# Three edits to a two-layer graph network: groups of x, one more early product, the order of the last group

## The chip, the core and the metric

The kernel runs on one core of a Trainium2 chip. Its engines run side by side, each with a queue of its own, and wait for each other by semaphores: PE multiplies matrices and writes to PSUM, DVE and ACT work element by element, POOL issues the gathers (indirect DMAs that fetch rows by index), SP issues the other DMAs. The metric is the time of one execution on the device in microseconds, as the median of several runs.

## The reference

x has N = 6250 rows (nodes) of D = 512, float32; src and dst are the E = 100,000 edges, sorted by dst. What is computed:

```python
h = jnp.maximum(_layernorm(x, axis=-1), 0.0)
# norm = -dinv[src] * dinv[dst], dinv = 1/sqrt(degree by src), 0 without edges
def prop(h):
    return jax.ops.segment_sum(h[src] * norm[:, None], dst, num_segments=N)
h = h @ W1_0 + prop(h) @ W1_1 + b1
h = _layer_norm(h, gamma, beta)
h = jnp.where(h >= 0, h, 0.01 * h)
return x + h @ W2_0 + prop(h) @ W2_1 + b2
```

So each of two layers multiplies the nodes' own rows by one matrix (W0 below) and the sums over their edges by another (W1), both 512 x 512.

## The kernel before, in words

**Tiles.** Nodes lie in NB = 49 blocks of 128 rows (the last has 106). Edges lie in NC = 782 chunks of 128. A chunk is fetched by one gather of 128 rows of 2 KB (L393 of `gather_to`) into one of R = 57 places in SBUF, in turn: chunk t goes into place `order[t % 57]`. Sixteen places are extra ones, the other 41 hold blocks 0 to 40 of x at first; the blocks behind them hold x too, and later, from the middle of layer 1, the second layer's weights.

**Sums.** Four lists of chunks make a group: list q of group g has three chunks of its own and the next list's first, so a full group is 16 products of a 128 x 32 selection matrix `sel` (made by DVE in `choose`, L504 and L515) with a gathered chunk, in `sums` (L527). The profile shows each float32 product as two records. The four lists write to four column groups of PE and lie side by side there. There are NS = 66 groups: group 0 has one list, the groups 1 to 64 have four, and group 65 has four lists of 4, 4, 4 and 2 chunks (771 to 774, 774 to 777, 777 to 780, 780 and 781), so 14 products and 28 records. ACT copies a group's sums to `agg` (L530).

**Blocks.** The rows of a group are nodes in order, but not aligned with blocks. `place` (L533 on) turns them into a block's transposed sums: for every group that may hold rows of the block (`inside[i]`, two or three groups) DVE writes a 0/1 matrix `there` (L540) and PE multiplies it with the group's `agg` in four parts (L543, eight records). DVE then scales the result into aT (L594). `own` transposes the block's own rows (L466) and ACT copies them (hT, L468). `dense` makes hT times W0 and aT times W1 in one PSUM tile (L478), and `finish` adds the bias, normalises, and stores: in layer 1 to a table tab[1] in DRAM, which layer 2 gathers from, and to h_tab; in layer 2 to the output.

**Order.** PE, POOL and SP issue in the order of the program; DVE's and ACT's order comes from the scheduler. For every group g the program issues the gathers up to chunk 3 * unit[g] + 57, the places of the blocks that are due, the sums of g, and the dense products of those blocks. A gather waits until the sums have used the chunk that lay in its place. The first gather of layer 2 needs all of tab[1]. Blocks 38 to 48 are due at groups 54, 55, 56, 58, 59, 60, 62, 63, 64, and, for 47 and 48, after the loops of groups 64 and 65; at groups 53 and 57 no block is due.

**Early blocks.** For three blocks, `EARLY`, W0 is not multiplied in `dense` but in `early`, at group 55 for block 46, 57 for 47 and 59 for 48, behind the sums and dense products of that group. Their rows are loaded two groups before (`load_early`) into tiles `pre`, one for each early block, which then hold the product with its bias until `finish` adds it.

**The start.** x is loaded into its places in groups of blocks (L165 on); ACT makes the sums and squares of the first 41 blocks, DVE counts degrees until some 85 us. When the scale of every row is known (93.9 us), `make_table` writes the normalised x of each group in place, on ACT (L407) or DVE (L404 and L405), and SP writes it to tab[0] in DRAM (L408). The first 60 chunks (RAW) are gathered from raw x, not from that table, and are normalised in SBUF: `find` and `look_up` (L418 to L444: PE, DVE, then ACT) fetch each row's scale. A gather into a place that holds a block of x waits until that block's group has been written to tab[0], so chunk 16 + i waits for the group of block i. Chunks from 60 on wait for the whole table.

Before the first group, `usual_path` makes table group 0 and group 1 on ACT, between them the loads for the first two blocks, and four look-ups. Then, at group 0:

```python
more_tables(1, [DVE])
gather_to(layer, RE + groups[3][0])
```

Then come the sums of group 0, the next table group (DVE and ACT by turns, block by block), a look-up, and all other table groups.

Of the kernel before, what the change touches and what calls it, by code (L numbers as in the profile page):

```python
# [8 lines left out]
F32 = mybir.dt.float32  # L9
# [10 lines left out]
P = 128  # L20
# [9 lines left out]
RE = 16  # L30
# [9 lines left out]
def gnn_kernel(  # L40
# [36 lines left out]
    NB = -(-N // P)  # L77
# [4 lines left out]
    NC = -(-E // P)  # L82
# [3 lines left out]
    NS = -(-NU // NQ)  # L86
# [65 lines left out]
    for ids, fill, name in ((src, 0, "src_c"), (dst, NO_NODE, "dst_c")):  # L152
        t = ep.tile([P, NG, P], I32, name=name)
# [11 lines left out]

    groups, i = [], 0
    while i < NB:
        n = min(NB - i, (2, 6, 8)[len(groups)] if len(groups) < 3 else 7)
        groups.append((i, n))
        i += n  # L170
    xs = []
    for i0, n in groups:
        t = places[:, i0 : i0 + n, :]
# [32 lines left out]
    with tc.tile_pool(name="turn", bufs=1) as wp, tc.tile_pool(  # L206
        name="turn_ps", bufs=2, space=bass.MemoryType.PSUM
# [17 lines left out]
    for (i0, n), t in zip(groups, xs):  # L225
        n = min(n, NB - LAST - i0)
# [13 lines left out]
    with tc.tile_pool(name="deg", bufs=1) as dp, tc.tile_pool(name="onehot", bufs=2) as ohp, tc.tile_pool(  # L240
        name="deg_ps", bufs=1, space=bass.MemoryType.PSUM
# [10 lines left out]
        for g in range(EJ // (2 * GJ)):  # L252
            hot = []
            for s, n, name in ((s_lo, LO, "lo"), (s_hi, HI, "hi")):
                t = ohp.tile([EP, GJ, n, 2], BF, name=name)
# [23 lines left out]
    with tc.tile_pool(name="fold", bufs=1) as dp, tc.tile_pool(  # L279
        name="fold_ps", bufs=1, space=bass.MemoryType.PSUM  # L280
# [27 lines left out]
    with tc.tile_pool(name="turn", bufs=1) as wp, tc.tile_pool(  # L308
        name="turn_ps", bufs=1, space=bass.MemoryType.PSUM
# [50 lines left out]
def usual_path(tc, have):  # L360
# [5 lines left out]
                          "minus unsorted ln dinv sdinv bias1 bias2 gam bet unseen unit N E D NB NC NU NS KD rows places "  # L366
                          "order groups xs sc pick src_lo src_hi p_id dup").split())
    AHEAD = 2
    EARLY = {NB - 3: NS - 11, NB - 2: NS - 9, NB - 1: NS - 7}
    ACT = mybir.EngineType.Activation  # L370
    R = len(order)
    UN = STEP * P * N / E
# [7 lines left out]
    with ExitStack() as es:  # L380
        pool = es.enter_context(tc.tile_pool(name="main", bufs=2))
# [5 lines left out]
        def zr(t):  # L387
            return places[:, order[t % R], :]

        def gather_to(layer, end):  # L390
            nonlocal gathered
            for t in range(gathered, min(end, NC)):
                nc.gpsimd.indirect_dma_start(  # L393
                    out=zr(t), out_offset=None, in_=x if layer == 0 and t < RAW else tab[layer],
                    in_offset=bass.IndirectOffsetOnAxis(ap=sidx[:, t : t + 1], axis=0))
            gathered = max(gathered, min(end, NC))

        def make_table(g, engines):

            i0, n = groups[g]  # L400
            for j in range(n):
                i, v = i0 + j, xs[g][:, j, :]
                if engines[i % len(engines)] == DVE:
                    nc.vector.tensor_scalar(v, v, sc[:, 0, i : i + 1], sc[:, 1, i : i + 1], op0=OP.mult, op1=OP.add)  # L404
                    nc.vector.tensor_scalar_max(v, v, 0.0)  # L405
                else:
                    nc.scalar.activation(v, v, AF.Relu, bias=sc[:, 1, i : i + 1], scale=sc[:, 0, i : i + 1])  # L407
            nc.sync.dma_start(tab[0][i0 * P : (i0 + n) * P, :].rearrange("(i p) d -> p i d", p=P), xs[g])  # L408
# [43 lines left out]
        def load(layer, i):  # L452

            if i not in EARLY:
                load_h(layer, i, "h", AHEAD)
# [25 lines left out]
        def load_early(layer, i):  # L481
            load_h(layer, i, "pre", len(EARLY))
            pre[i] = own_h[i]
            if layer == 1:
                load_x(i)
# [33 lines left out]
        def sums(g, sel, chunk):  # L519

            n = len(chunk)
            ps = psum.tile([P, D], F32, name="ps")
            todo = [(s, q) for s in range(SPAN) for q in range(n) if s < len(chunk[q])]
            if g == NS - 1:
                todo.sort(key=lambda t: chunk[t[1]][t[0]])
            for s, q in todo:
                nc.tensor.matmul(ps[q * Q : (q + 1) * Q, :], sel[:, q, s, :], zr(chunk[q][s]), start=(s == 0),  # L527
                                 stop=(s == len(chunk[q]) - 1))
            agg[g] = pool.tile([P, D], F32, name="agg", bufs=3)
            nc.scalar.activation(agg[g][: n * Q], ps[: n * Q], AF.Copy)  # L530

        def place(i, some):

            r = rows[i]
            if i not in placed:
                placed[i] = psum.tile([P, KD, P], F32, name="aT_ps", bufs=1)
            for g in some:
                m = Q * (unit[g + 1] - unit[g])
                there = pool.tile([P, P], F32, name="there", bufs=3)
                nc.vector.tensor_scalar(there[:m, :r], iota_r[:m, :r], node_of[:m, g : g + 1], -(1.0 + i * P),  # L540
                                        op0=OP.subtract, op1=OP.is_equal)
                for kc in range(KD):
                    nc.tensor.matmul(placed[i][:, kc, :r], agg[g][:m, kc * P : (kc + 1) * P], there[:m, :r],  # L543
                                     start=(g == inside[i][0] and kc == 0),
                                     stop=(g == inside[i][-1] and kc == KD - 1))

        def finish(layer, i, v):
            r = rows[i]
            v = v[:r]
            if layer == 1:  # L550
                o = pool.tile([P, D], F32, name="t")
                if i in EARLY:
                    nc.vector.tensor_add(o[:r], v, pre.pop(i)[:r])
# [6 lines left out]
            if i < NB - 1:  # L560
                nc.vector.tensor_add(v, v, pre.pop(i)[:r] if i in EARLY else bias1[:r])  # L561
            st = pool.tile([P, 6], F32, name="st")
# [21 lines left out]
        def turn(layer, i):  # L584

            r = rows[i]
            if layer == 1 and i not in EARLY:
                load_x(i)
            if i + AHEAD < NB:
                load(layer, i + AHEAD)  # L590
            hT = None if i in EARLY else own(layer, i)
            place(i, [g for g in inside[i] if i < NB - 1 or g == NS - 1])
# [61 lines left out]
        for i in range(AHEAD):  # L654
            load(0, i)
        make_table(1, [ACT])
        for k in range(RE // 4):
            look_up("u_ps")
            find("ps")
        tables = 2  # L660

        def more_tables(n, engines):
            nonlocal tables
# [4 lines left out]
        for layer in range(2):  # L668
            if layer == 1:
                gathered = 0  # L670
                for i in range(AHEAD):
                    load(layer, i)
            i = 0
            for g in range(NS):
                if layer == 0 and g == 0:
                    more_tables(1, [DVE])
                    gather_to(layer, RE + groups[3][0])
                else:
                    gather_to(layer, STEP * unit[g] + R)
                if layer == 0 and g == NS // 2:  # L680
                    for k, w in enumerate((W2_1, W2_0)):
                        nc.sync.dma_start(w_late[:, k], w.rearrange("(k p) d -> p k d", p=P))
                if layer == 0:
                    look_up("hT_ps")
                    find("hT_ps")
                    assert looked >= min(RAW, STEP * unit[g + 1] + 1)
                due = []
                while inside[i].stop <= g:
                    due.append((i, turn(layer, i)))
                    i += 1  # L690
                if g == NS - 2:
                    for k, (hT, aT) in due:
                        dense(layer, k, hT, aT)
                    due = []
                sums(g, *(chosen if g == NS - 1 else choose(g)))
                if layer == 0:
                    if g == 0:
                        more_tables(1, [DVE, ACT])
                    look_up("hT_ps")
                    find("hT_ps")  # L700
                    if g == 0:
                        more_tables(len(groups), [DVE, ACT])
                for k, (hT, aT) in due:
                    dense(layer, k, hT, aT)
                if layer == 0:
                    look_up("hT_ps")
                    find("hT_ps")
                    if g == NS // 2:
                        check()
                for k, at in EARLY.items():  # L710
                    if g == at - 2:
                        load_early(layer, k)
                    if g == at:
                        early(layer, k)
                if g == NS - 2:
                    chosen = choose(NS - 1)
                    if layer == 0:
                        r = rows[NB - 1]
                        started[NB - 1] = psum.tile([P, D], F32, name="u_ps")
                        nc.tensor.matmul(started[NB - 1][:r], ident[:r, :r], pre[NB - 1][:r], start=True, stop=False)  # L720
                    while inside[i].stop < NS:
                        dense(layer, i, *turn(layer, i))
                        i += 1
                    assert i == NB - 1
                    place(i, inside[i][:-1])
            dense(layer, i, *turn(layer, i))
# [322 lines left out]
```

## Time and profile before

| | |
|---|---|
| median of the runs | 2531.47 us (2527.57, 2531.47, 2532.97) |
| the profiled execution | 2509.83 us, its span 2508.0 us |
| mean granted clock of PE | 0.885 |
| layer 1: first gather into a place that held x | 99.18 us |
| layer 1: last gather | 1239.7 us |
| layer 2: first gather | 1310.31 us |
| layer 2: last gather | 2440 us |
| a gather on POOL (L393) | 0.95 us busy |
| sums of a full group, 32 records, while POOL pauses | 3.57 us |
| a block's place, 24 records, while POOL pauses | 2.7 us |
| W0 or W1 of one block, 8 records, while POOL pauses | 3.5 to 3.7 us |

The profile is one execution. Its rows name an instruction by line, engine, operation and tiles; "idle before" says how long the engine had nothing to run just before, and which event ended that. The chain is followed back from the last instruction: each step goes to what released it. "Issue" is idle time for which the profile shows no cause. PE's rows show when a product is started; their ends are modelled, and when another engine sees the result can be later.

### The profile page before, as it was taken

How to read it: one execution, taken by the hardware profiler on the slowest of the kernel's cores; microseconds unless marked ns; L12 is line 12 of the kernel's file. 1: busy time of each engine (PE TensorE's matmuls, PEld its weight loads, DVE VectorE, ACT ScalarE, POOL GpSimd, SP SyncE). 2: the span in 40 equal slices, each digit the busy share in tenths (PEclk: the TensorE clock that was granted, in tenths of full speed). 3: DMA queues.
4: the chain of work that ended last, by engine and by line, in shares of the span. 5: the costliest groups of instructions: out<-in, count | busy, mean ns of one | idle time of the engine just before them, and what ended most of it. 6: DMA issues, size and time to landing. Idle time of an engine off the chain costs nothing.

```text
span 2508.0 us, 24149 instructions
## 1 busy us (share of the span) xinstructions
PE 1948.0 (78%) x9101; PEld 913.8 (36%) x9101; DVE 691.2 (28%) x1381; ACT 377.3 (15%) x694; POOL 1496.6 (60%) x1577
## 2 busy tenths in 40 slices
PE   5617788688888888887874568887888888688888
PEld 4414343243334334333430233333333333343344
DVE  8923223232324223323340011111111111111221
ACT  8724111111111111112110000000000000000000
POOL 4175666666666666665507566666666666666660
PEclk8757899899999999999996679998998989889999
DMA  9395677767677677776627567677676777677770
GB/s 341 102 336 152 213 228 217 213 209 223 211 220 256 208 223 222 215 224 214 188 70 214 178 201 225 208 229 221 218 226 212 221 212 221 211 214 236 220 225 28
DMA packets 198947, 527.08 MB, mean 210 GB/s; under 512 B 31864, under 2 KB 46019, under 8 KB 198822
## 3 DMA queue, kind: packets, MB, share of 16 engines
q0 software_dynamic: 125120, 410.09, 53.7%
q1 hardware_dynamic: 73702, 115.36, 13.3%
q8 instruction: 73, 1.20, 0.2%
q14 instruction: 52, 0.43, 0.1%
HBM read 474.06 MB, written 51.27 MB: 209 GB/s over the span
## 4 chain that ended last, share of the span: by engine, by line
PE 67%; issue 17%; another core or an unknown queue 5%; DVE 5%; POOL 3%; DMA 2%; ACT 1%; SPq 0%; POOLq 0%; DVEq 0%; ACTq 0%
PE u_ps L478 26%; PE ps L527 25%; PE aT_ps L543 13%; POOL places L393 3%; PE hT_ps L466 2%; DMA places<-tab,sidx 1%; DVE hi L256 1%; DVE lo L256 1%; DVE places L404 0%; DVE places L405 0%; ACT agg L530 0%; PE both_ps L262 0%; PE u_ps L433 0%; PE hT_ps L433 0%
## 5 line engine op out<-in xcount | busy, mean ns | idle before, releaser
L393 POOL DMA_INDIRECT places<-tab,sidx x1504 | 1421.8, 945 | 844.3 <-issue 395.5
L527 PE MATMUL ps<-places,sel 128*32 128x512 f32 x4168 | 734.2, 649 | 158.8 <-issue 108.9
L543 PE MATMUL aT_ps<-there,agg 128*128 128x128 f32 (+2 forms) x2320 | 381.7, 313 | 207.4 <-issue 191.8
L543 PEld LDWEIGHTS aT_ps<-there,agg 128*128 128x128 f32 (+1 forms) x2320 | 340.2, 222 | 245.7 <-issue 224.0
L527 PEld LDWEIGHTS ps<-places,sel 128*32 128x32 f32 x4168 | 165.9, 117 | 647.6 <-issue 585.7
L515 DVE TENSOR_TENSOR sel<-dlx,nodes_ps 128x512 f32<-128x512 f32 (+3 forms) x134 | 89.7, 671 | 804.9 <-remote 513.6
L530 ACT ACTIVATE agg<-ps 128x512 f32<-128x512 f32 (+1 forms) x132 | 78.7, 596 | 1206.2 <-remote 632.1
L478 PE MATMUL u_ps<-w,hT 128*128 128x512 f32 (+1 forms) x392 | 189.7, 616 | 25.4 <-issue 15.9
L478 PE MATMUL u_ps<-places,hT 128*128 128x512 f32 (+1 forms) x392 | 185.7, 611 | 14.7 <-ACT hT L468 7.6
L478 PE MATMUL u_ps<-w,aT 128*128 128x512 f32 (+1 forms) x392 | 181.1, 596 | 13.8 <-issue 9.8
L478 PE MATMUL u_ps<-places,aT 128*128 128x512 f32 (+1 forms) x392 | 177.9, 593 | 6.6 <-issue 4.2
L540 DVE TENSOR_SCALAR there<-iota_r,node_of 128x128 f32<-128x128 f32 (+1 forms) x290 | 84.1, 293 | 340.0 <-remote 184.3
L478 PEld LDWEIGHTS u_ps<-w,hT 128*128 128x128 f32 (+1 forms) x392 | 71.7, 192 | 140.6 <-issue 121.0
L478 PEld LDWEIGHTS u_ps<-places,hT 128*128 128x128 f32 (+1 forms) x392 | 70.7, 190 | 127.3 <-issue 119.4
L478 PEld LDWEIGHTS u_ps<-w,aT 128*128 128x128 f32 (+1 forms) x392 | 73.1, 189 | 114.3 <-issue 108.9
L478 PEld LDWEIGHTS u_ps<-places,aT 128*128 128x128 f32 (+1 forms) x392 | 73.9, 189 | 101.7 <-issue 98.7
L594 DVE TENSOR_TENSOR aT<-aT_ps,to 128x512 f32<-128x512 f32 (+1 forms) x98 | 67.3, 687 | 150.9 <-PE ps L527 117.5
L393 POOL DMA_INDIRECT places<-in_x_dram,sidx x44 | 44.2, 1005 | 90.3 <-ACT places L407 58.8
L468 ACT ACTIVATE hT<-hT_ps 128x512 f32<-128x512 f32 (+1 forms) x98 | 58.1, 593 | 246.7 <-PE hT_ps L466 69.8
L561 DVE TENSOR_TENSOR u_ps<-u_ps,bias 128x512 f32<-128x512 f32 x46 | 32.2, 700 | 190.7 <-PE u_ps L478 86.1
L555 DVE TENSOR_TENSOR u_ps<-u_ps,bias 128x512 f32<-128x512 f32 x46 | 32.1, 699 | 183.2 <-PE u_ps L478 92.1
L463 ACT ACTIVATE h<-h,ln 128x512 f32<-128x512 f32 x46 | 37.2, 812 | 256.4 <-issue 131.0
(138 smaller groups left out, 963.7 us busy)
## 6 DMA issues: line engine op xcount, KB each, us to landing
places<-tab,sidx POOLq DMA_INDIRECT x1504
tab<-t SPq DMA_DIRECT2D x48, 256.0 KB
h_tab<-g SPq DMA_DIRECT2D x48, 256.0 KB
xt<-in_x_dram SPq DMA_DIRECT2D x48, 256.0 KB
out_dram<-t SPq DMA_DIRECT2D x48, 256.0 KB
h<-in_x_dram SPq DMA_DIRECT2D x46, 256.0 KB
h<-h_tab SPq DMA_DIRECT2D x46, 256.0 KB
places<-in_x_dram SPq DMA_DIRECT2D x4, 1792.0 KB
```

The lines of the kernel that those rows point to most:

```text
L256: nc.vector.tensor_tensor(t, s[:, g * 2 * GJ : (g + 1) * 2 * GJ].rearrange("p (j s) -> p j s", s=2)[:, :, None, :] .to_broadcast([EP, GJ, ...
L393: nc.gpsimd.indirect_dma_start(out=zr(t), out_offset=None, in_=x if layer == 0 and t < RAW else tab[layer], in_offset=bass.IndirectOffsetO ...
L463: nc.scalar.activation(h[:r], h[:r], AF.Relu, bias=ln[:r, 1, i : i + 1], scale=ln[:r, 0, i : i + 1])
L466: nc.tensor.transpose(ps[:, kc, :r], h[:r, kc * P : (kc + 1) * P], ident[:r, :r])
L468: nc.scalar.activation(hT[:, :, :r], ps[:, :, :r], AF.Copy)
L478: nc.tensor.matmul(u_ps[:r], hT[:, kc, :r], w[:, kc, :], start=(start and kc == 0), stop=(stop and kc == KD - 1))
L515: nc.vector.tensor_tensor(sel[:, q : q + k, :w, :], of, node[:, q : q + k, None, :].to_broadcast([P, k, w, Q]), op=OP.is_equal)
L527: nc.tensor.matmul(ps[q * Q : (q + 1) * Q, :], sel[:, q, s, :], zr(chunk[q][s]), start=(s == 0), stop=(s == len(chunk[q]) - 1))
L530: nc.scalar.activation(agg[g][: n * Q], ps[: n * Q], AF.Copy)
L540: nc.vector.tensor_scalar(there[:m, :r], iota_r[:m, :r], node_of[:m, g : g + 1], -(1.0 + i * P), op0=OP.subtract, op1=OP.is_equal)
L543: nc.tensor.matmul(placed[i][:, kc, :r], agg[g][:m, kc * P : (kc + 1) * P], there[:m, :r], start=(g == inside[i][0] and kc == 0), stop=(g ...
L594: nc.vector.tensor_tensor(aT[:, :, :r], placed.pop(i)[:, :, :r], to.pop(i)[:, None, :r].to_broadcast([P, KD, r]), op=OP.mult)
```

## The change

Three things are changed, and one buffer is taken away.

First, x comes in groups of 2, 4, 4, 4 and five of 7 blocks, where it came in 2, 6, 8, four of 7 and one of 5. The three first groups (10 blocks) are made into the table by ACT before group 0, where two (8 blocks) were; the group that DVE makes before the sums of group 0 has 4 blocks, where it had 8. The gathers issued there end at chunk 30 instead of 32, since `groups[tables][0]` is 14 where `groups[3][0]` was 16. SP issues nine loads of x and nine table writes instead of eight.

Second, block 45 becomes an early block: its W0 is multiplied at group 53, its rows are loaded at group 51. `pre` has four tiles instead of three, and `there` two instead of three, so the third matrix of a block can be written when PE has used the first.

Third, the products of group 65 are sorted by max(chunk, 779) instead of by chunk. The first eleven, chunks 771 to 779, then keep the order of the other groups (first chunk of every list, then the second, and so on, as far as they are below 780); chunk 780 follows for lists 3 and 2, and chunk 781.

```diff
-        n = min(NB - i, (2, 6, 8)[len(groups)] if len(groups) < 3 else 7)
+        n = min(NB - i, (2, 4, 4, 4)[len(groups)] if len(groups) < 4 else 7)
...
-    EARLY = {NB - 3: NS - 11, NB - 2: NS - 9, NB - 1: NS - 7}
+    EARLY = {NB - 4: NS - 13, NB - 3: NS - 11, NB - 2: NS - 9, NB - 1: NS - 7}
...
             if g == NS - 1:
-                todo.sort(key=lambda t: chunk[t[1]][t[0]])
+                todo.sort(key=lambda t: max(chunk[t[1]][t[0]], NC - 3))
...
-                there = pool.tile([P, P], F32, name="there", bufs=3)
+                there = pool.tile([P, P], F32, name="there", bufs=2)
...
         make_table(1, [ACT])
+        make_table(2, [ACT])
         for k in range(RE // 4):
             look_up("u_ps")
             find("ps")
-        tables = 2
+        tables = 3
...
                     more_tables(1, [DVE])
-                    gather_to(layer, RE + groups[3][0])
+                    gather_to(layer, RE + groups[tables][0])
```

## The prediction

> **What bounds the kernel now.** I read the page's rows of busy time and the chain first, then the timelines of POOL, PE and DVE, then the chain stretch by stretch.
>
> ```profile
> PE 1948.0 (78%) x9101; PEld 913.8 (36%) x9101; DVE 691.2 (28%) x1381; ACT 377.3 (15%) x694; POOL 1496.6 (60%) x1577
> ...
> PE 67%; issue 17%; another core or an unknown queue 5%; DVE 5%; POOL 3%; DMA 2%; ACT 1%; SPq 0%; POOLq 0%; DVEq 0%; ACTq 0%
> ...
> L393 POOL DMA_INDIRECT places<-tab,sidx x1504 | 1421.8, 945 | 844.3 <-issue 395.5
> L527 PE MATMUL ps<-places,sel 128*32 128x512 f32 x4168 | 734.2, 649 | 158.8 <-issue 108.9
> ```
>
> PE carries two thirds of the chain, but it and POOL hold each other. A gather takes 0.95 us and 0.30 us of issue, 1.25 us in all; POOL runs 10 to 14 of them, stops for 2.2 to 2.9 us until the sums of a group free places, and runs again. Sums that lie four groups apart start at 741.9, 810.0, 879.3, 950.0, 1018.1 and 1088.9: 68 to 71 us for 48 gathers, which alone take 60 us. PE's own work for the same four groups, at the durations it has while POOL pauses, is some 45 us; in the later part of each POOL run it gets one record started every 0.7 or 1.4 us. No view names what holds it. So three stages are judged apart: the start, where POOL waits for x's places; the steady part; and the ends of both layers, after the last gather, where PE is alone and every microsecond of it counts.
>
> The start, in POOL's timeline (chunks 18, 24 and 30):
>
> ```profile
> 100.42 0.95 POOL L393 DMA_INDIRECT places<-in_x_dram,sidx  x1 [0.30 <-issue]
> 113.77 0.95 POOL L393 DMA_INDIRECT places<-in_x_dram,sidx  x1 [12.40 <-ACT places L444]
> ...
> 128.23 1.03 POOL L393 DMA_INDIRECT places<-in_x_dram,sidx  x1 [6.63 <-DVE ac L442]
> ...
> 136.47 0.94 POOL L393 DMA_INDIRECT places<-in_x_dram,sidx  x1 [0.30 <-DVE both L439]
> ```
>
> POOL lost 12.40 and 6.63 us here. The releasers named had other work; what POOL waited for are the table's writes, as a place may be overwritten only when its block of x has been written out: group 1 (6 blocks) was issued at 103.90 and landed at 111 to 113, group 2 (8 blocks, made by DVE) was issued at 117.16 and landed at 127.45. From 128.23 POOL runs unbroken to 189.9. The chain behind it:
>
> ```profile
> 141.73 18.01 another core or an unknown queue
> 159.76 0.69 DVE sel L515
> 160.45 20.99 another core or an unknown queue
> ```
>
> That is PE, held back under POOL's long run; the sums of group 2 start only at 200.23, after it.
>
> The end of layer 1, in the chain:
>
> ```profile
> 1258.21 0.44 PE hT_ps L466 x4
> ...
> 1279.77 3.57 PE ps L527 x32
> ...
> 1291.52 5.38 PE ps L527 x28
> ```
>
> **1. Groups of x.** The loads: ACT's statistics end at 78.2, after which ACT is idle until 92; DVE's counting, to 85, sets that stage, so loads of another size are worth 0. If that cover went, one load's wait (1.43 us before group 1's statistics) is the price. One x load and one table write more cost SP 0.37 us each (the median of L408's DMAs), beside other work. The tables: chunks 18 to 29 now need groups 1 to 3, of 4 blocks each. Group 1's write, 1 MB, is issued at 103.9; 1.5 MB took 7.08 us to its main part, so it lands between 108.6 (in proportion) and 111.0 (same time). Groups 2 (ACT, ready by 104.9) and 3 (DVE, whose first four pairs of L404 and L405 end at 104.3) follow at once and land, by the same bytes per time, by 112 and 115; chunk 26 would reach group 3 only at about 119. So POOL resumes at 110 to 112 instead of 113.77 and makes twelve gathers, to 125 or 127. Chunk 30 needs group 4 (7 blocks): DVE makes it after the first selection, to about 121 (7 pairs at 0.46 + 0.34 us), and its write lands about 5 to 6 us later, 126.5. Chunk 30 starts at 126.5 to 128 instead of 136.47: 8.5 to 10 us earlier. All of this reaches the end only if PE's sums follow. The sums of group 1 (138 to 142) and the look-ups have so far run before PE was held back; if that begins earlier, part of them falls into it. Ends: −10 and +3 (ACT's later table takes one block more, and the sums of group 1 may be caught). I take −6, nearer the gain, because the gathers up to chunk 72 need nothing from PE but the sums of groups 0 and 1.
>
> The Trainium skill, "DMA: Bandwidth & Descriptors", Bandwidth, speaks against smaller writes: it wants at least 1 MiB in a DMA and gives 1 MB 6.15 us, 78% of peak. By that figure group 1 lands at 110.1, in between my two bounds; the sum goes by the bounds.
>
> **2. Block 45's W0 in group 53.** In each layer's tail four transposes (0.44 us) and eight records of W0 (1264.83 to 1268.37, 3.53 us) go: −4.0 us, all on the chain, since POOL's last gather is at 1239.7 and DVE and ACT wait for PE. They come back after the sums of group 53 (1088.9 to 1092.6), where no block is due. PE there does 4.1 us more and waits for ACT's copy of hT between; in the three blocks treated so already that wait was 3.21, about 1 and 2.19 us. The price in the lock-step: a stretch of four groups without such a block takes 69.0 to 69.3 us, with one 72.6, with two 71.3 or 69.7, alike in both layers: 3.5, 1.1 and 0.3 us for each, 1.6 on average. So −2.4 us a layer, −4.8 in all. Ends: free, −8; all of 4.1 + 3.2 us paid, +3.3 a layer, +6.6. The block's load, at group 51, has two groups (some 35 us) to land, in a buffer of its own; behind it on SP stand only loads for later blocks.
>
> **3. Last group.** Fourteen products take 5.38 us, sixteen of a full group 3.57. The old order (by chunk) sends one list's products behind each other: counting four column groups that run side by side and one queued each gives six rounds of 0.89 us, 5.4. The new order takes the first eleven by turn of the lists, then chunks 780 and 781: four rounds, 3.57. −1.8 us a layer, −3.6 in all. Every gather landed some 45 us before (1243 against 1291.5), so the order makes nothing wait. Late next is the copy by ACT (0.60), as before. Ends: −4.4 (another half round each) and 0.
>
> **4. Two buffers for `there`.** This adds a wait. With three, a block's matrices are all written before its place begins: the lead is 9 us at least. With two, the third matrix waits until PE has used the block's first. DVE's order stays, and at the spot where it now waits it waited before for that same use (there for the next block's matrix); so DVE loses nothing and what stands behind (`sel`, aT, the finish) moves only if PE does. PE could lose. I compared, for all blocks, the end of the write that stands at that spot now with the start of PE's third part. Around 1050, in PE's timeline and in DVE's:
>
> ```profile
> 1047.97 2.84 PE L543 MATMUL aT_ps<-there,agg 128*128 128x128 f32 x24
> ```
> ```profile
> 1051.22 0.48 DVE L540 TENSOR_SCALAR there<-iota_r,node_of 128x128 f32<-128x128 f32 x1 [0.75 <-PE aT_ps L543]
> ...
> 1055.46 0.29 DVE L540 TENSOR_SCALAR there<-iota_r,node_of 128x128 f32<-128x128 f32 x1 [2.88 <-remote]
> ...
> 1059.69 0.69 DVE L594 TENSOR_TENSOR aT<-aT_ps,to 128x512 f32<-128x512 f32 x1 [3.27 <-remote]
> ```
>
> PE's rows start the third part at 1049.76, the matrix would be there at 1051.70: 1.9 us late, which is also the median of 89 such places, 227 us in all. That is the upper end. But the same rows show PE's uses *complete* far behind the records: DVE sees the first done at 1051.2, the second at 1055.4, the third at 1059.7. A matrix that comes at 1051.70 is 3.8 us ahead of the second's completion. In 79 of 89 places it is ahead by 0.3 us or more (median 1.2); in ten it comes with it, and costs about one write, 0.28 us. I take +2 (0 to +227), by the rows of completion.
>
> On PE's running ahead, the Trainium skill, "TensorE: Matmul & The Clock Gate", Back-to-back issue gap, speaks of a 64-deep reorder window; 33 records (with weight loads, 66) lie here between a use and its completion, which fits, and a wait inside a block takes this lead from PE.
>
> **Sum.** −6 − 4.8 − 3.6 + 2 = −12.4. The profiled execution (2509.83 us, span 2508.0) becomes 2497; it lies 21.6 us under the median of the runs, 2531.47, so I put the same difference there: 2519.
>
> **Rivals.** *A, given back (22%):* PE's hold in the start begins as much earlier as POOL does, and group 53 pays its work in full instead of a fourth; only the last group stays, with the waits: −3.6 + 2 = −1.6, 2530. For it: a hold that has no named cause may go with the gathers' number. Against: the steady part pays 1.6 us for such work. *B, slower (20%), the third matrix:* PE's lead over its completions is what carries it through POOL's runs, and each mid-block wait is paid at the rate of PE work in group 53's like, 1.6 of 6.1 us, a fourth: 227 / 4 = 57. 2531.5 − 14.4 + 57 = 2574. It decides from a sixteenth of the 227 on (14.4 us). For it: the late arrivals recur in nearly every block. Against: the completion rows. *C, everything (8%):* start −10, W0 free: −10 − 8 − 3.6 = −21.6, 2510. The forecast itself (2513 to 2526) has 50%.
>
> **How the numbers follow.** A measurement tells 0.2% (5 us) from no change. Faster by more: forecast and C less what reaches the edge, 55%; within: A, 22%; slower: B and the worst of A, 23%. Range: below to C with 2 us of the runs' spread, 2508; above into B to a tenth of its late arrivals plus the open start (2531.5 − 8 + 23), 2547, which leaves 15% above and 4% below.
>
> **What would show it.** Chunk 30's gather near 127 and the sums of group 2 near 192 (start); the last group's 28 records in 3.6 us; no W0 between 1258 and 1270 less the shift, and groups 52 to 56 within 73 us; PE rows of L543 with idle time released by DVE L540 below 5 us in all. Wrong if four steady groups take over 70 us throughout (B), or if the sums of group 2 stay near 200 (A).

## The result and the profile after

The changed kernel takes 2596.96 us (2583.93 to 2603.68, four runs), the kernel before 2529.52 us beside it (2519.07 to 2532.97): a ratio of 1.027, 95% interval 1.0241 to 1.0298. The prediction was 2519 us, faster; the change is 67 us slower. Its profiled execution took 2594.12 us, with a span of 2592.3 us and a mean granted clock of 0.846 where it was 0.885.

The page of the changed kernel, the same rows as shown of before and the row of the places' products beside them:

```profile
PE 1903.8 (73%) x9101; PEld 919.2 (35%) x9101; DVE 692.4 (27%) x1377; ACT 380.9 (15%) x698; POOL 1504.4 (58%) x1577
...
PE 57%; issue 17%; another core or an unknown queue 13%; DVE 7%; POOL 3%; DMA 2%; ACT 1%; SPq 0%; POOLq 0%; ACTq 0%; DVEq 0%
...
L393 POOL DMA_INDIRECT places<-tab,sidx x1504 | 1425.6, 948 | 936.6 <-issue 394.1
L527 PE MATMUL ps<-places,sel 128*32 128x512 f32 x4168 | 658.7, 703 | 77.1 <-issue 40.3
L543 PE MATMUL aT_ps<-there,agg 128*128 128x128 f32 (+2 forms) x2320 | 411.5, 327 | 412.2 <-issue 286.1
```

and that last row on the page of the kernel before:

```profile
L543 PE MATMUL aT_ps<-there,agg 128*128 128x128 f32 (+2 forms) x2320 | 381.7, 313 | 207.4 <-issue 191.8
```

The last number ahead of the arrow is PE's idle time just before these instructions. Before L543 it was 207.4 us and is 412.2; before L527 it was 158.8 and is 77.1. So PE now stands still longer ahead of the places, and less in the sums behind them, which makes up for part of it. The table says where the 84 us between the two profiled executions arose, by the start of a group's sums:

| sums of group | layer 1, before | after | later by | layer 2, later by |
|---|---|---|---|---|
| 2 | 200.2 | 186.1 | −14.1 | |
| 5 | 249.6 | 245.4 | −4.2 | 51.3 |
| 21 | 531.4 | 545.9 | 14.5 | 55.2 |
| 37 | 810.0 | 842.7 | 32.7 | 72.0 |
| 53 | 1088.9 | 1133.6 | 44.7 | 77.9 |
| 61 | 1232.8 | 1286.5 | 53.7 | 88.4 |
| 65 | 1291.4 | 1343.2 | 51.8 | 86.0 |

The start is earlier, the ends of both layers shrink, and between them the kernel loses a little in most stretches of groups. From group 33 to group 53 of layer 1, four groups take 71.8 to 78.5 us where they took 68.1 to 70.8: the prediction's sign for its rival B. What is lost shows best in layer 2, in PE's timeline and in DVE's (start, duration, what, and idle before it):

```profile
1676.76 1.95 PE L543 MATMUL aT_ps<-there,agg 128*128 128x128 f32 x16
1684.21 2.04 PE L543 MATMUL aT_ps<-there,agg 128*128 128x128 f32 x8 [5.50 <-issue]
1686.18 5.77 PE L527 MATMUL ps<-places,sel 128*32 128x512 f32 x32
...
1699.29 1.95 PE L543 MATMUL aT_ps<-there,agg 128*128 128x128 f32 x16
1707.32 2.05 PE L543 MATMUL aT_ps<-there,agg 128*128 128x128 f32 x8 [6.08 <-issue]
```
```profile
1679.45 0.69 DVE L556 TENSOR_TENSOR t<-u_ps,xt 128x512 f32<-128x512 f32 x1
1683.78 0.28 DVE L540 TENSOR_SCALAR there<-iota_r,node_of 128x128 f32<-128x128 f32 x1 [3.64 <-remote]
```

By its rows, PE works through the first two of a block's three matrices by 1678.7 and then has nothing to do. DVE is idle from 1680.14; it writes the third matrix only at 1683.78, because it sees only then that PE has used the first, whose products started at 1676.76 and need 0.9 us. That signal is some 6 us late. DVE's write takes 0.28 us, and PE goes on 0.15 us behind it. DVE itself is not what is held up: the trace also has the times of PE's semaphore updates, and one stands at 1683.76, 0.02 us ahead of the write. Of the 125 such writes of this profile that come over 1 us late (counted as under experiment 1), 123 begin within 0.03 us of an update.

At the end of layer 1 the last group is as predicted:

```profile
1342.28 1.04 PE L543 MATMUL aT_ps<-there,agg 128*128 128x106 f32 x8
1343.24 3.66 PE L527 MATMUL ps<-places,sel 128*32 128x512 f32 x28
```

One thing has to be said ahead of the experiments. They ran on two chips, and the kernel before does not take the same time on both: on the one, **chip A** below, 2101 us; on the other, **chip B**, 2516 to 2529 us. On which chip the result was measured is not recorded; its kernel before, at 2529.52 us, takes the time of chip B. Every ratio below is against the kernel before on the same chip.

### The profile page after: what moved, and what is told of

The parts are those of the page before. It is cut to its first block, busy times and chain, and to the rows that moved or that the text cites. A ratio compares the mean times of both kernels' runs of the same rounds, so it can differ in the third digit from the quotient of the medians.

```text
span 2592.3 us, 24151 instructions
## 1 busy us (share of the span) xinstructions
PE 1903.8 (73%) x9101; PEld 919.2 (35%) x9101; DVE 692.4 (27%) x1377; ACT 380.9 (15%) x698; POOL 1504.4 (58%) x1577
## 4 chain that ended last, share of the span: by engine, by line
PE 57%; issue 17%; another core or an unknown queue 13%; DVE 7%; POOL 3%; DMA 2%; ACT 1%; SPq 0%; POOLq 0%; ACTq 0%; DVEq 0%
PE u_ps L478 22%; PE ps L527 20%; PE aT_ps L543 12%; POOL places L393 3%; PE hT_ps L466 2%; DMA places<-tab,sidx 2%; DVE lo L256 1%; DVE hi L256 1%; DMA h<-in_x_dram 1%; DVE there L540 0%; DVE u_ps L561 0%; DVE st L564 0%; DVE sel L515 0%; ACT agg L530 0%
## 5 line engine op out<-in xcount | busy, mean ns | idle before, releaser
L527 PE MATMUL ps<-places,sel 128*32 128x512 f32 x4168 | 658.7, 703 | 77.1 <-issue 40.3
L543 PE MATMUL aT_ps<-there,agg 128*128 128x128 f32 (+2 forms) x2320 | 411.5, 327 | 412.2 <-issue 286.1
L543 PEld LDWEIGHTS aT_ps<-there,agg 128*128 128x128 f32 (+1 forms) x2320 | 360.1, 233 | 457.1 <-issue 416.5
L527 PEld LDWEIGHTS ps<-places,sel 128*32 128x32 f32 x4168 | 151.6, 127 | 508.2 <-issue 461.2
L478 PE MATMUL u_ps<-w,hT 128*128 128x512 f32 (+1 forms) x392 | 196.9, 637 | 30.2 <-ACT hT L468 14.8
L466 PEld LDWEIGHTS hT_ps<-ident,h 128*128 128x128 f32 x360 | 43.9, 143 | 69.7 <-issue 69.4
```

Of the source, the lines that this page charges most:

```text
L466: nc.tensor.transpose(ps[:, kc, :r], h[:r, kc * P : (kc + 1) * P], ident[:r, :r])
L478: nc.tensor.matmul(u_ps[:r], hT[:, kc, :r], w[:, kc, :], start=(start and kc == 0), stop=(stop and kc == KD - 1))
```

## The experiments

The theory after the result (W in the expectations): two buffers make PE wait inside every block for a signal that comes late while POOL gathers, and the whole loss is this. Rivals: the new start shifts how groups fall on POOL's runs (S), or group 53 costs far more than forecast (E).

**1. Two buffers alone, chip A.**

```diff
-                there = pool.tile([P, P], F32, name="there", bufs=3)
+                there = pool.tile([P, P], F32, name="there", bufs=2)
```

> The kernel before with two buffers for there instead of three, nothing else. Theory W (the wait): PE stops inside each block's place until DVE has seen the use of the block's first matrix, and that signal comes some microseconds late while POOL gathers; the whole loss of the change comes from here. The change lost 67 us with gains in it that were forecast at 14 us, so this kernel should be at 2529 + 70 to 85 = 2600 to 2615, ratio 1.028 to 1.034, with four steady groups at 71 to 73 us. Rival S (the start): the new groups of x shift how the groups of edges fall on POOL's runs, and the loss is theirs; then this kernel stays within 2524 to 2535. Rival E (group 53 and the moved W0): also 2524 to 2535 here.

Measured: 2101.05 us, ratio 0.9997 (0.9988 to 1.0006). The theory's 70 to 85 us did not come, on a chip where the kernel before takes 2101 us. Its trace shows why: which event ended DVE's idle time before each `there`, in the view of that tile,

```profile
  PE aT_ps L543: 44.6, 72
  ACT agg L530: 9.6, 6
```

and the page's row of the places' products:

```profile
L543 PE MATMUL aT_ps<-there,agg 128*128 128x128 f32 (+2 forms) x2320 | 280.1, 277 | 4.0 <-ACT agg L530 3.8
```

DVE waited 0.6 us at a time for PE, and PE 4.0 us in all before 2320 instructions. Whenever DVE's write waited for PE, it began 0.04 us after the end of the products that released it; not one came 1 us late. In the profiles of the prediction and of the result the same interval has a median of 4.4 us in the kernel before (109 of 114 over 1 us) and 5.2 us in the changed one, counted where DVE stood idle over 0.3 us, from 230 to 1300 us and from 1480 us on. On chip A PE does not creep without a named cause either; where it stops in the sums, it is mostly for a gather to land (228.1 us in 153 waits). POOL gathers from 127.0 to 1076.2 without a pause, 758 gathers, and that sets the time.

**2 to 4. The other three parts alone, chip A.** The groups of x with what goes with them; the order of the last group; and block 45 as an early block with three buffers for `there` (room made by a constant, `diff`, moved to the memory of the start).

```diff
+        n = min(NB - i, (2, 4, 4, 4)[len(groups)] if len(groups) < 4 else 7)
...
+                todo.sort(key=lambda t: max(chunk[t[1]][t[0]], NC - 3))
...
+    EARLY = {NB - 4: NS - 13, NB - 3: NS - 11, NB - 2: NS - 9, NB - 1: NS - 7}
```

> The kernel before with only the new groups of x (2, 4, 4, 4, five of 7) and what goes with them. Theory W: no loss here; the prediction's term is -6 us, 2523 (ratio 0.9975), between -10 and +3. In the changed kernel the sums of group 2 started 14 us earlier and those of group 7 13 us later than before. Theory G (given back): the earlier start is lost again by group 8 and the time is 2527 to 2532. Rival S: 2580 or more.

> The kernel before with only the new order of the last group's products. Prediction's term: -1.8 us a layer, 28 records in 3.6 instead of 5.4 us, -3.6 us in all, 2526 (ratio 0.9986). Rival: ACT's copy or the next place ends the stretch anyway, no change (ratio 1.000).

> The kernel before with only block 45 made early at group 53; three buffers for there are kept (diff lies in the pool of the start and is made again where the general path needs it, which frees the 512 bytes). Prediction's term: -4.0 us a layer in the tail and +1.6 us at group 53, -4.8 us in all, 2525 (ratio 0.998), between -8 and +7. Rival E: the loss of the change is here, 2580 or more. Rival: group 53 pays the work in full, 2529 to 2536.

Measured: groups 0.9978 (0.9969 to 0.9987), −4.6 us; last group 0.999 (0.9981 to 0.9999), −2.1 us; early block 0.9976 (0.9967 to 0.9985), −5.0 us. None carries a loss there. In the first, POOL's two waits of the start are 9.90 and 1.60 us; in the kernel with only the last group changed, whose start is that of before, 11.77 and 4.37 us on this chip. The difference, 4.6 us, is as much as the kernel gained.

**5. All parts with three buffers, chip B.** The changed kernel, `there` with three buffers again (`diff` moved as above).

> The changed kernel with three buffers for there (diff lies in the pool of the start and is made again where the general path needs it, which frees the 512 bytes). Theory W: the loss is gone and the three other parts remain, -14 us by the prediction's terms, 2515 (ratio 0.9943); if the start gives its gain back, -8, 2521. Rivals S and E: 2580 or more.

Measured: 2496.01 us against 2516.03, ratio 0.9918 (0.9886 to 0.995), −20 us. The loss is gone and the three parts stay, so S and E fall. This version is faster than both kernels on chip B. Chunk 30's gather and the one ahead of it, in POOL's timeline:

```profile
125.52 1.52 POOL L393 DMA_INDIRECT places<-in_x_dram,sidx  x1 [0.30 <-issue]
128.97 1.38 POOL L393 DMA_INDIRECT places<-in_x_dram,sidx  x1 [1.93 <-DVE places L404]
```

128.97 instead of 136.47. The sums of groups 3 to 14 of layer 1 start 9 to 11 us earlier than before, those of groups 28 to 53 some 12 to 14 us. These are differences of single profiles. In layer 2 the lead falls from some 20 us to about nothing at group 52 and is 7 at the end. The profiled execution of the kernel before was 22 us faster than the median of its runs, so the −20 us rest on the medians and not on these profiles.

**6 and 7. One buffer, and four, chip B.**

> The kernel before with one buffer for there: the second matrix waits for the first's use and the third for the second's, two round trips in a block instead of one. Theory W: more than the loss with two buffers, near its double if both signals come as late, 2529 + 130 to 170 = 2660 to 2700; waits of PE before the place of 400 us or more. Theory L (only lateness against a fixed cover counts: DVE answers at once and PE has the second part to do meanwhile): little more than with two, 2600 to 2630.

> The kernel before with four buffers for there (diff moved as in the others to make room). With three every matrix is written 9 us or more before its use. Theory W: no change, ratio 0.998 to 1.002. Rival: the write order on DVE matters too and a longer lead gains, ratio below 0.997.

Measured: one buffer 2683.91 us, ratio 1.0683 (1.0643 to 1.0722), +168 us, twice the price of two; PE idle before L543 573.6 us by the page. Four buffers 1.0003 (0.9978 to 1.0029), nothing; since `diff` was moved there too, that move is worth nothing either. The price goes with the number of waits inside a block: none with three or four, one with two, two with one.

**8 and 9. Two buffers alone, and the changed kernel, together on chip B.**

> The first experiment's kernel again (the kernel before with two buffers for there). On the first chip the kernel before took 2101 us and this one the same; on the chip of the prediction the kernel before takes 2530 us, and there PE's results are seen by DVE microseconds late while POOL gathers. Theory W: it depends on that lateness. On a chip where the kernel before takes 2500 us or more this one is 70 to 90 us slower (ratio 1.028 to 1.036); where it takes 2100 us, no change. Rival: two buffers never cost anything by themselves, and the loss needs the other edits beside them; then no change on either.

> The changed kernel itself. Where the kernel before takes 2100 us: the three gains as measured alone there, -4.6, -2.1 and -5.0, and nothing for the buffer: 2089 (ratio 0.9945). Where it takes 2500 us or more: slower again by 60 to 75 us (ratio 1.024 to 1.030).

Measured: two buffers alone 2603.7 us, ratio 1.0335 (1.0299 to 1.037), +81 us; the changed kernel 2594.64 us, 1.0287 (1.0252 to 1.0322), +72 us. So on this chip the one buffer costs more than the whole change does, and the other three parts give back 9 to 12 us. On the page of two buffers alone the row of the places' products shows the same idle time as in the changed kernel:

```profile
L543 PE MATMUL aT_ps<-there,agg 128*128 128x128 f32 (+2 forms) x2320 | 420.1, 332 | 415.6 <-issue 264.2
```

In its trace PE's idle time ahead of a matrix's first product, in the stretches from 230 to 1300 us and from 1480 on, is 290 us where it is 36 us before.

**10 and 11. Without the gathers, and with plain copies, chip B.** Both with two buffers. The first leaves out all gathers from chunk 60 of layer 1 on, so the sums use old contents. The second replaces them by copies of 128 consecutive rows, so the sums use the wrong rows:

```diff
+                if layer == 1 or t >= RAW:
+                    at = t % (NB - 1) * P
+                    nc.sync.dma_start(zr(t), tab[layer][at : at + P, :])
+                    continue
```

> The kernel with two buffers for there, with the gathers of chunk 60 and on in layer 1 and all of layer 2's left out, so the sums use what lies in the places. If POOL's gathers delay what others see of PE, then without them DVE sees the first matrix used within 0.1 us, PE has no waits within a block, and four steady groups take PE's 45 to 50 us, 1500 to 1700 us in all, on any chip. Rival (PE itself is slow on that chip, its clock or its weights): late signals and 0.7 us steps stay.

> The kernel with two buffers for there, with the same gathers replaced by plain DMAs of 128 consecutive rows (the same bytes and the same rows of 2 KB, wrong nodes), issued by SP. If the traffic into SBUF delays PE's signals, they stay late on a chip where the kernel before takes 2500 us. If the gathers' descriptors, which POOL writes, do it, they come within 0.1 us and PE has no waits within a block. Where the kernel before takes 2100 us both give no lateness.

Measured: 1691.75 and 1786.74 us (one run each), on the chip where the kernel before took 2522.53 beside them. In both, DVE's write comes 0.04 us after PE's products, always. With plain copies, PE's timeline of a block:

```profile
821.98 0.60 PE L470 MATMUL hT_ps<-ident,h 128*128 128x128 f32 x4
822.42 2.84 PE L547 MATMUL aT_ps<-there,agg 128*128 128x128 f32 x24
825.19 3.64 PE L531 MATMUL ps<-places,sel 128*32 128x512 f32 x32
```

Two buffers, three matrices, no gap: PE's own work on the second matrix is cover enough when the signal is prompt. PE is not slow on this chip as such, since without gathers it needs 1691.75 us. The DMA engines move over 300 GB/s in most slices of the kernel with plain copies, more than the 210 of before, so it is not the amount of traffic that makes signals late.

**12. Two buffers with more cover, chip B.** The third matrix's products move behind the sums of the group.

```diff
+                due = [(k, (hT, last_list(k, aT) if g < NS - 2 else aT)) for k, (hT, aT) in due]
```

> Two buffers for there, and the third matrix's products of a block moved behind the sums of the group (until group 63), so PE has those sums, 3.6 us, between asking for the third matrix and needing it. On a chip where the kernel before takes 2500 us the signal comes 4.9 us late in the median (7.8 at the ninetieth percentile), of which the second list now covers 0.9 and the sums would cover 3.6. Theory W (the price is the lateness that no work covers): most of the 81 us is gone, 2530 to 2555, ratio 1.003 to 1.013. Theory Q (the price is the loss of PE's lead at any point inside a block): little changes, 2580 to 2605. Where the kernel before takes 2100 us: no change, within 0.3%.

Measured: 2560.77 us against 2528.56, ratio 1.0107 (1.0033 to 1.0181): +32 us by the medians, +27 by the ratio, instead of +81. The ratio is within W's range, though its interval reaches beyond it; Q's range, 1.020 and more, lies outside. PE's timeline shows a block whose late signal the sums hide:

```profile
1659.04 1.95 PE L543 MATMUL aT_ps<-there,agg 128*128 128x128 f32 x16
1660.91 3.64 PE L527 MATMUL ps<-places,sel 128*32 128x512 f32 x32
1664.49 1.16 PE L543 MATMUL aT_ps<-there,agg 128*128 128x128 f32 x8
```

and PE's waits show what is late next:

```profile
PE ps L527 <- issue: 132.4, 149, 2.5
PE u_ps L478 <- DVE aT L607: 111.7, 23, 21.3
PE aT_ps L543 <- issue: 85.8, 110, 3.1
```

aT, the round trip that follows the third matrix, now has only W0's products for cover; in the kernel before this wait was 5.2 us.

**13 and 14. Half the rows; POOL busy without gathers, chip B.** Both with two buffers. The first gathers 64 rows instead of 128 from chunk 60 on, so half of each place is old; the second sets the place to a constant on POOL instead.

> Two buffers, and gathers of 64 rows instead of 128 from chunk 60 on (the other half of each place keeps what it held). Where signals are late with full gathers: if the number of rows a gather writes out sets the lateness, signals come much earlier, under 2 us in the median, and PE's waits in L543 fall below half of 415 us; if POOL's being busy at all sets it, lateness stays near 4.9 us as long as POOL runs.

> Two buffers, and from chunk 60 on a memset of the place on POOL instead of a gather, so POOL is busy and waits for the same places, but writes out no descriptors and moves nothing. If POOL's work as such delays PE's signals, they stay late where the kernel before takes 2500 us; if only its gathers do, DVE sees the first matrix used after 0.04 us and PE has no waits within a block.

Measured (one run each): half the rows 2643.83 us, signals late by 4.27 us in the median, PE idle before the places 395.0 us: as late as with whole gathers, which take POOL nearly as long (0.902 against 0.945 us). The constants 1698.49 us, signals 0.04 us behind, PE idle 1.6 us before all of these products. POOL is busy 0.53 us for each constant there, not 0.95. So on this chip it is not POOL's being busy with any work, not the bytes and not the number of rows above 64 that makes PE's signals late; it takes gathers on POOL. What of a gather does it is not separated: its issue on POOL, the queue it goes through, or its scattered rows, since the plain copies differ in all three.

**15. The changed kernel, once more, chip B.**

> The changed kernel once more beside them. Where the kernel before takes 2500 us: ratio 1.024 to 1.032. Where it takes 2100 us, the three gains measured alone there remain, 2089, ratio 0.9945.

Measured: 2586.78 us against 2528.56, ratio 1.022 (1.016 to 1.0281), +58 us, a little less than expected. The whole change was not run on chip A. The four parts measured alone there add to −12 us, which would be 2089; that sum is an estimate and not a result.

## Why the prediction was wrong

**The step that failed is part 4,** "I take +2 (0 to +227), by the rows of completion". The prediction had seen that the third matrix would be written after PE wanted it, 1.9 us in the median and 227 us in 89 places, and set that aside because the second matrix's use was *seen* complete later still: a matrix "is 3.8 us ahead of the second's completion". It read the gap between a record and its signal as work that PE still had to do, so that the third products would have stood behind it anyway, and a wait inside the gap would be free. The runs showed that it is not free: on chip B two buffers alone cost 81 us. PE's idle time ahead of the matrices grew by 254 us (36 to 290), so about a third of the standing still was not made up afterwards. Rival B had priced a fourth, 57 us; the forecast and B stood at 50% and 20%, and the range ended at a tenth.

That the gap is not all work can be read from PE's semaphore updates in the changed kernel. The signal of the third products in the lines above comes at 1690.91, 4.65 us after their row's end, and those of the next three quarters of the sums at 1690.95, 1691.04 and 1691.13. On chip A the same three signals follow each other at 0.86 to 0.99 us, the time of the work between them. So the third products must have been done by about 1688.4 (an estimate from these numbers), some 2.5 us ahead of their signal. The same bound comes out in 15 of the 46 places of this profile where the third part's signal is over 1 us late and the sums follow at once. Whether PE's results or only their signals are late in the rest of the gap stays open.

The Trainium skill, "Perfetto Trace Analysis", Tensor Engine Instruction, says that the shown end of a matrix product is estimated from its size, and that the semaphore is updated only when PSUM has acknowledged all bytes. The rows agree that shown end and signal are two things: 0.04 us apart on chip A, 4.4 us in the median in the profile of the kernel before. That section gives no figure for the gap, and no run here shows in which of its steps the microseconds pass.

The prediction counts 33 records between a use and its completion; in the trace of the kernel before at most 31 start between them. The sum does not use this number.

**Part 1, the start, was right in its mechanism, its size probably a little low on chip B.** In experiment 5 POOL resumed at 111.44 (forecast 110 to 112), chunk 30 started at 128.97 (126.5 to 128), 7.5 us earlier, and the sums of group 2 at 175.4 (192). −6 was taken, because PE's hold might begin earlier. It did not take the gain back: the 9 to 11 us last through group 14. On chip A the part alone gave −4.6 us; on chip B it was not run alone. Rival A falls with it. In the changed kernel the sums of group 2 started 14 us earlier, and the buffer had eaten that by group 7.

**Part 2, block 45, came out at the forecast's number, in part by luck.** −4.8 us forecast, −5.0 measured on chip A. But the 1.6 us that group 53 was to pay a layer had been read from the lock-step of PE and POOL, which chip A does not show, and from stretches of four groups that were said to take 69.0 to 69.3 us. Single such stretches of that profile, from group 5 to group 53 of both layers, take 67.7 to 75.6 us, too wide a spread for a price of 1.6 us. In experiment 5 the tail of layer 1 is 3.4 us shorter between the sums of groups 63 and 64, and no loss is seen between groups 52 and 58.

**Part 3, the last group, was right in its mechanism:** 3.7 us for 28 records instead of 5.4, in both layers; −3.6 us forecast, −2.1 (−0.2 to −4.0) measured.

The sum without part 4 was −14.4 us. Measured: −20 (−13 to −29) on chip B with all three parts, −12 on chip A as the sum of the parts alone.

**What should have led to B.** The profile of before had the sign: in the later part of each POOL run PE gets one record started every 0.7 or 1.4 us, and "No view names what holds it". This creeping comes and goes with the late signals: neither is seen on chip A, without gathers, with plain copies or with constants. So it has most likely the same cause, though no run shows that apart, and the wait adds a round trip PE–DVE–PE in the middle of that stretch. The price of a new round trip is bounded by the measured lateness of such round trips in the place where it is put, less the work that stands between; how much of that reaches the end, here a third, only a run can tell.

## What to carry to other kernels

A buffer taken away is paid with a round trip between two engines. Price it by how late signals come in that stretch, from the idle time of the engine that waits for them, and let only work that the waiting engine really has in between count as cover; that the signals of other work come later still is no cover. When space is short, take it from a constant that is no longer needed before you take a buffer from a loop: here 512 bytes of each partition decided between −20 and +67 us.

## What the runs showed of the hardware

The same kernel takes 2101 us on one chip and 2516 to 2529 us on another; no third was tried. On the slower, DVE sees PE's results 4.4 us late in the median (7.5 at the ninetieth percentile) while POOL gathers, and PE then starts one record every 0.7 or 1.4 us; some 2.4 us after POOL's last gather the signals are back. With gathers of half the rows it is the same (4.27 us, with two buffers); with plain copies of the same bytes by SP, with POOL setting constants, or with no gathers, signals take 0.04 us on that same chip. On the faster chip they take 0.04 us with the gathers too. In one block of the changed kernel at least some 2.5 us of the delay, by the estimate above, are the signal's alone. What differs between the chips, what of a gather delays the signals, and whether PE's results are held up as well, stays open.
